# Four graph layers on one core: a bias, a norm and a mask of the last stage in other places

## The chip, the cores and the metric

The kernel runs on one core of a Trainium2 chip. The metric is the device time of one execution in microseconds; the runs shown are the median of three. The engines are called as in the profile: PE (TensorE matmuls, with PEld for its weight loads), DVE (VectorE), ACT (ScalarE), POOL (GpSimd) and SP (SyncE, which issues the transfers).

## What is computed

The input is 128 small graphs of 128 nodes with 128 features, and a 0/1 adjacency matrix for each. Four layers follow each other, every one on a normed and rectified copy of its input, and every one added back to it. The last two are attention layers:

```python
def _L2_gnn_ref(x, adj, W, b, a):          # 4 heads of 32
    h = (x @ W + b).reshape(Bb, Nn, H, D)
    e = e_i[:, :, None, :] + e_j[:, None, :, :]      # h times the halves of a
    e = jnp.where(e > 0, e, 0.2 * e)
    e = jnp.where(adj[..., None] > 0, e, NEG)
    attn = jax.nn.softmax(e, axis=2)
    out = jnp.einsum('bijh,bjhd->bihd', attn, h)
...
def _L3_gnn_ref(h, adj, W, a):             # one head of 128
    ...                                    # the same without b
    return jax.nn.elu(h_prime)

# layers 2 and 3
h = jnp.maximum(_layernorm(x, axis=-1), 0.0)
x = x + _L2_gnn_ref(h, adj, ...)
h = jnp.maximum(_layernorm(x, axis=-1), 0.0)
x = x + _L3_gnn_ref(h, adj, ...)
```

Layer 0 sums over neighbours, and layer 1 is an attention whose scores come from the pairwise differences of all nodes; it takes most of the time. Two batch norms over all graphs stand in layer 1, so the work falls into three stages.

## The kernel before, in words

The 128 graphs are worked in 32 groups of G = 4; a tile of a group is 128 partitions by 4 x 128. The first stage does layer 0 and the pairwise products of layer 1, up to the first batch norm. The second stage reads these products back, forms the scores and attention of layer 1, and gathers the second batch norm. It also prepares, in `brief`, the small constants of the last stage. The last stage does the rest of layer 1 and layers 2 and 3. It comes in two forms: `attention` for the inputs at hand, and `last_stage`, a fallback that a branch takes for others and that does not run here.

`attention(n_th, g, fourth)` breaks one group into some 60 named steps, each with an engine, a planning cost and the names of the steps that it follows. `_ranked` then lists the steps of all groups in one order for each engine: a step is chosen when its predecessors, its buffers (`BUFS`, and the PSUM banks `ONE` and `TWO`) and its engine are free in the plan, ties and near choices being settled by a rank. The rank of a step is `EVERY * n_th + RANK3[name]`, and `JOIN3[n_th]` is the planned time from which a group may start. The engines then run their lists in that order, each instruction waiting for its own inputs.

The steps that matter here, in the order of one group:

- `off` (POOL, L1474): the mask of missing edges from the byte matrix `M8[g]`, 1 where there is no edge. PE multiplies it by `no_edge` and adds the product to the scores (L1619, L1659).
- `y`, `yl`, `po`, `x1`: the end of layer 1; ACT scales, DVE rectifies, PE multiplies, DVE adds (L1477 to L1488).
- `layer(2, ...)` and later `layer(3, ...)`: `mv` takes the moments on DVE (L1501, L1503); `rs` forms the inverse deviation and the negated, scaled mean `nb` on POOL in four small instructions (L231, L232, L1507, L1508); `h` scales and rectifies on ACT in four instructions of 128x128 (L1513); `pt` transposes on PE (L1519), `hT` copies back on ACT (L1588); `pr` multiplies by the weights (L1528), with the two score columns of each head beside the features; `v` copies the score columns out (DVE, L1536) and `wr` the values (ACT, L1551, L1554).
- In layer 2, `pr` starts with two more products for each group, `ones3` by `b_parts` (L1525): the bias, split into three bf16 parts, with its share in the score columns.
- `sp` (POOL, L1567, L1569) splits the scores into three bf16 pieces, `pe` transposes them (L1574), `left` and `right` spread them, and `ps` forms all pair scores (L1616, L1619; L1656, L1659).
- `e` and `em`: two exps on ACT (L1602, L1603) and the larger of them on DVE (L1606); `w` or `pv` multiplies by the values (L1629, L1665); `o` divides by the sums (L1644, L1670). `x2` adds layer 2's result to x, with -1 for the later ELU (L1649); `ex`, `x3`, `x4` and `out` finish layer 3.

`brief` makes `b_parts` in the second stage with its inner functions `joined` and `piece`, twelve small DVE instructions. In the second stage `normed` of `chain` also adds a constant row `bt` to x on POOL (L997) and makes a cap out of the byte matrix by product and sum (L995).

Of the kernel before, what the change touches and what calls it, by code (L numbers as in the profile page):

```python
# [9 lines left out]
F32 = mybir.dt.float32  # L10
I32 = mybir.dt.int32
BF16 = mybir.dt.bfloat16
U8 = mybir.dt.uint8
AF = mybir.ActivationFunctionType
# [50 lines left out]
         ("right3", "right3", "ps"), ("e", "e", "pv"), ("o3", "o", "ex x3"), ("ex", "ex", "x4"))  # L65
EVERY = 16.7
RANK3 = {"off": 260, "y": 228, "yl": 425, "po": 78, "x1": -85, "mv2": 311, "rs2": 127, "h2": 106, "pt2": -67,
         "hT2": -32, "pr2": 29, "v2": -191, "w12": 226, "wr2": -506, "sp2": 154, "pe2": -472, "left2": -44,
         "right2": -400, "ps0": -41, "e0": -28, "e0m": -161, "w0": 61, "e1": 118, "e1m": -270, "w1": 25,
         "o1": -270, "ps2": -33, "e2": 78, "e2m": 74, "w2": 73, "e3": -271, "e3m": -457, "w3": -134, "o3": 98,  # L70
         "x2": -10, "mv3": -52, "rs3": -133, "h3": 71, "pt3": -106, "hT3": 27, "pr3": 92, "v3": -161, "w13": -36,
         "wr3": 125, "sp3": -261, "pe3": -83, "left3": 4, "right3": -32, "ps": -287, "e": 21, "em": -17,
         "pv": -160, "o": -8, "ex": 360, "x3": 119, "x4": 187, "out": 299, "lz": 146, "lx": -73}
JOIN3 = (20, 2, 0, 0, 1, 2, 28, 29, 0, 13, 49, 23, 67, 94, 51, 151,
         131, 78, 137, 199, 221, 127, 166, 143, 241, 183, 223, 276, 237, 165, 178, 294)

# [93 lines left out]
def tile_gnn_stack(ctx: ExitStack, tc: tile.TileContext, a: dict, out: bass.AP):  # L170
# [10 lines left out]
    def fixed(shape, dtype=F32, name=None):  # L181

        if name not in K:
            K[name] = const.tile(shape, dtype, name=name)
        return K[name]
# [78 lines left out]
    def over_group(t):  # L264
        return t[:, None, :].to_broadcast([P, G, P])

    def two_stages(general):
# [535 lines left out]
        with tc.tile_pool(name="c1", bufs=1, reuse_waits="tile") as c1, \  # L803
                tc.tile_pool(name="p1", bufs=2, reuse_waits="tile") as p1:
            prepared, scored = {}, {}
            room["turns"] = p1
            small_ones, pair = [], []
# [74 lines left out]
            def at(slot, place, work):  # L882
                jobs.setdefault((slot, place), []).append(work)
# [206 lines left out]
            no_edge = fixed([P, P], BF16, name="no_edge")  # L1090
            b_parts = fixed([3, P + 8], BF16, name="b_parts")
            ones3 = fixed([3, P], BF16, name="ones3")
            own_h = fixed([P, 4], F32, name="own_h")
            own_k = fixed([P, 4], F32, name="own_k")

            def brief():
# [3 lines left out]
                def scratch():  # L1100
                    for left, names in ((selfb.rearrange("p g t -> p (g t)"),
                                         (("wt0", P), ("wt1", P), ("left", P + 8), ("add_b", 8), ("bounds", 24),
                                          ("square", 16), ("bound", 1), ("by_batch", 16), ("tops", NG + 3))),
                                        (c1.tile([P, P + 8 + 3 * (P // 2 + 4)], F32, name="brief"),
                                         (("part", P + 8), ("one0", P // 2 + 4), ("one1", P // 2 + 4), ("one2", P // 2 + 4)))):
                        for name, n in names:
                            t[name], left = left[:, 0:n], left[:, n:]
                    nc.gpsimd.memset(t["bounds"], 0.0)
                    nc.gpsimd.memset(t["part"], 0.0)
                    nc.gpsimd.memset(ones3, 1.0)  # L1110
                    nc.vector.tensor_copy(ident_b, ident)
                    nc.vector.tensor_scalar(no_edge, ident, NEG_EDGE, None, op0=OP.mult)

# [7 lines left out]
                def copied():  # L1121
                    for i in range(2):
                        nc.scalar.copy(t[f"wt{i}"], t["pt"][:, i, :])
                    nc.scalar.copy(t["add_b"], t["pt"][:, 2, 0:8])

# [16 lines left out]
                def compared():  # L1142
                    nc.vector.tensor_copy(t["bounds"][:, 0:10], t["pn"][:, 0, 0:10])
                    nc.vector.tensor_tensor(t["bounds"][:, 16:24], t["add_b"], t["add_b"], OP.mult)
                    nc.vector.tensor_reduce(t["bound"], t["bounds"], AX.X, OP.max)
# [21 lines left out]

                def joined():
                    nc.vector.tensor_copy(t["left"][0:3, 0:P], b_2[0:3, :])
                    nc.vector.tensor_copy(t["left"][0:3, P:], t["add_b"][0:3, :])  # L1170


                def piece(n):
                    left, part, one = t["left"][0:3, :], t["part"][0:3, :], t[f"one{n}"].bitcast(BF16)[0:3, 0:P + 8]
                    nc.vector.tensor_copy(one, left)
                    nc.vector.tensor_tensor(left, left, one, OP.subtract)
                    nc.vector.scalar_tensor_tensor(part, one, ident[0:3, n:n + 1], part, op0=OP.mult, op1=OP.add)
                    if n == 2:
                        nc.vector.tensor_copy(b_parts, part)

                def owners():
# [12 lines left out]
                at(end + 4, "l", compared)  # L1198
                at(end + 1, "l", joined)
                for n in range(3):  # L1200
                    at(end + 5 + n, "l", lambda n=n: piece(n))
                at(end + 8, "l", owners)
# [30 lines left out]
    w2x, w3x, wtyT, b_2, b_2c, a2, a3, ident_b, no_edge, \  # L1233
        ones3, b_parts, own_h, own_k, scale2, bias2, bounded, flag = (
        K[n] for n in ("w2x", "w3x", "wtyT", "b_2", "b_2c", "a2", "a3", "ident_b", "no_edge", "ones3", "b_parts", "own_h", "own_k", "scale2", "bias2", "bounded", "flag"))

    def last_stage():
        nonlocal psum, banks
        with tc.tile_pool(name="c2", bufs=1) as c2, tc.tile_pool(name="p2", bufs=5) as p2, \
# [84 lines left out]
            def group(g):  # L1324
# [7 lines left out]
                off = p2.tile([P, G, P], BF16, name="off")  # L1332
                nc.gpsimd.tensor_scalar(off, M8[g], 0.0, None, op0=OP.is_equal)
                yield
# [47 lines left out]

                nc.vector.scalar_tensor_tensor(x, o, -1.0, x, op0=OP.add, op1=OP.add)
                yield
# [38 lines left out]
    with tc.If(nc.values_load(bounded, min_val=0, max_val=1) > 0) as cmp, \  # L1423
# [10 lines left out]
        def attention(n_th, g, fourth):  # L1434
# [38 lines left out]
            def masked():  # L1473
                nc.gpsimd.tensor_scalar(sb("off", [P, G, P], BF16), M8[g], 0.0, None, op0=OP.is_equal)  # L1474

            step("off", "Pool", 1.54, lx, masked)
            step("y", "ACT", 0.81, () if on_chip else ("lz",), lambda: nc.scalar.activation(  # L1477
# [13 lines left out]
            def layer(n, heads, wx, first):  # L1491
# [18 lines left out]
                def normed():  # L1510
                    h = sb("h", [P, G, P])
                    for k in range(G):
                        nc.scalar.activation(h[:, k, :], t["x"][:, k, :], AF.Relu, bias=t[nb][:, k:k + 1],  # L1513
                                             scale=t[rs][:, k:k + 1])
# [6 lines left out]
                def projected():  # L1521
                    pr = two(q("pr"), N)
                    if first:
                        for a in range(2):
                            nc.tensor.matmul(pr[:, a, :, :], ones3, b_parts[:, None, :].to_broadcast([3, 2, N]),  # L1525
                                             start=True, stop=False, skip_group_check=True)
                    for k in range(G):
                        nc.tensor.matmul(pr[:, k // 2, k % 2, :], t[q("hT")][:, k, :], wx, start=not first,  # L1528
                                         stop=True, skip_group_check=True)

                def scores():
                    v = sb(q("v"), [P, 2, G, heads])
                    for a in range(2):
                        v_a = v[:, :, 2 * a:2 * a + 2, :].rearrange("p s b h -> p b s h")
                        pr_a = t[q("pr")][:, a, :, P:].rearrange("p b (s h) -> p b s h", s=2)
                        nc.vector.tensor_copy(v_a, pr_a)  # L1536

# [41 lines left out]
                def right():  # L1579
# [5 lines left out]
                step(rs, "Pool", 1.85, (mv,), root)  # L1585
                step(q("h"), "ACT", 1.65, (rs,), normed)
                step(q("pt"), "PE", 0.65, (q("h"),), turned, takes=(q("pt"),))
                step(q("hT"), "ACT", 0.59, (q("pt"),), lambda: nc.scalar.copy(sb(q("hT"), [P, G, P]), t[q("pt")]),  # L1588
                     last=(q("pt"),))
                step(q("pr"), "PE", 1.50 if first else 1.15, (q("hT"),), projected, takes=("2" + q("pr"),))  # L1590
                step(q("v"), "DVE", 0.32, (q("pr"),), scores)
# [17 lines left out]
            for k in range(G):  # L1609
# [38 lines left out]

            step("x2", "DVE", 0.69, ("o3",), lambda: nc.vector.scalar_tensor_tensor(  # L1649
                t["x"], t["o2"], -1.0, t["x"], op0=OP.add, op1=OP.add))  # L1650

# [86 lines left out]
```

## Time and profile before

| | before |
|---|---|
| median of 3 runs | 2656.92 us (2652.68 to 2657.95) |
| the profiled execution | 2653.83 us |
| its span | 2652.0 us |
| last stage, from the first `y` to the last result on DVE | 2225.5 to about 2647 us |

The span is what the profiler sees between the first and the last instruction; the execution's own time is 1.8 us longer. A group row of the profile gives the line, the engine, the operation, output and input names with their sizes and the count; behind the first bar the busy time and the mean of one in ns, behind the second the idle time of the engine just before, and whose work ended it. A window row gives each engine's busy time and instructions in a stretch, the granted PE clock, the DMA share and the GB/s moved. A wait row says which engine waited at which line for which other, with total, count and longest. A row with three figures in ns gives the shortest, median and longest instruction.

### The profile page before, as it was taken

Reading aid. Unit: us, or ns where it says so; the run is one execution under the profiler, and the core shown is the slowest. Engines: PE = TensorE matmul, PEld = TensorE weight load, DVE = VectorE, ACT = ScalarE, POOL = GpSimd, SP = SyncE. Lnnn points to the kernel's source line nnn. Section 1 sums busy time; section 2 is a strip of 40 time slices with the busy share of each in tenths; the row PEclk is TensorE's granted clock in tenths of the full one; section 3 lists DMA queues with packets and bytes.
Section 4 is the critical chain, followed back from the end, with each engine's and each line's share of the span. In section 5 each row is a group of like instructions: output and inputs, shape, how many; then the busy total and the mean of one; then the engine's idle time right before and its main releaser. Section 6 shows DMA issues by size and latency. Waiting matters only on the chain. (4 is left out here: it accounts for less than half of the span.)

```text
span 2652.0 us, 41948 instructions
## 1 busy us (share of the span) xinstructions
PE 2425.3 (91%) x14521; PEld 1155.4 (44%) x14521; DVE 2468.8 (93%) x4740; ACT 2376.6 (90%) x2821; POOL 1693.7 (64%) x1628
## 2 busy tenths in 40 slices
PE   6999999999999999999998988888888887999997
PEld 3333333333333333333332444444444445777776
DVE  5999999999999999999998898888888897899997
ACT  5999999999999999999998978887777774999997
POOL 6999999999999999999996110101110014666663
PEclk8999999999999999999999999999999997999999
DMA  3555555555555555555556899999999982021211
GB/s 102 199 207 210 209 212 207 214 208 211 207 210 207 210 207 210 207 210 210 207 210 227 339 408 410 409 410 409 410 409 410 398 345 81 21 69 57 66 36 34
DMA packets 185426, 611.43 MB, mean 231 GB/s; under 512 B 31987, under 2 KB 99702, under 8 KB 121718
## 3 DMA queue, kind: packets, MB, share of 16 engines
q1 hardware_dynamic: 184768, 608.50, 59.8%
q8 instruction: 118, 1.93, 0.3%
q14 instruction: 102, 0.84, 0.1%
q10 hardware_dynamic: 438, 0.17, 0.0%
HBM read 312.58 MB, written 296.03 MB: 229 GB/s over the span
## 5 line engine op out<-in xcount | busy, mean ns | idle before, releaser
L328 POOL TENSOR_TENSOR d<-xe 128x2048 f32<-128x2048 f32 x256 | 1073.5, 4203 | 36.5 <-PE hp L338 34.5
L338 PE MATMUL hp<-d,w1T 128*64 128x512 f32 x4096 | 994.2, 601 | 57.0 <-ACT z L352 54.0
L376 ACT ACTIVATE d<-d 128x2048 f32<-128x2048 f32 x384 | 733.5, 1922 | 20.2 <-POOL d L328 19.8
L328 DVE TENSOR_TENSOR d<-xe,xp 128x2048 f32<-128x2048 f32 x256 | 580.1, 2266 | 6.9 <-POOL xe L423 4.0
L352 ACT COPY z<-hp 128x1024 f32<-128x1024 f32 x512 | 519.0, 1015 | 9.7 <-PE hp L338 4.6
L338 PEld LDWEIGHTS hp<-d,w1T 128*64 128x64 f32 x4096 | 277.2, 136 | 558.7 <-issue 454.7
L997 POOL TENSOR_TENSOR x<-x,bt 128x512 f32<-128x512 f32 x27 | 39.1, 1449 | 555.6 <-DMA x<-x 447.7
L366 DVE BATCH_NORM_STATS2 st<-z 128x6 f32<-128x512 f32 x512 | 347.6, 679 | 6.1 <-ACT z L352 6.0
L367 DVE BATCH_NORM_STATS2 st<-z 128x6 f32<-128x512 f32 (+1 forms) x512 | 329.2, 643 | 0.0
L945 DVE SCALAR_TENSOR_TENSOR z<-z 128x2048 f32<-128x2048 f32 x128 | 297.8, 2327 | 6.3 <-ACT z L915 6.3
L926 ACT ACTIVATE zr<-z,bias,scale 128x2048 f32<-128x2048 f32 x128 | 267.3, 2089 | 7.8 <-DVE bias L797 7.8
L915 ACT ACTIVATE z<-z,bias,scale 128x2048 f32<-128x2048 f32 x128 | 267.0, 2087 | 0.0
L341 PE MATMUL hp<-both_t,xw 128*64 128x512 f32 x1024 | 265.2, 592 | 0.0
L892 PE MATMUL ps<-z,w2z 128*32 128x512 f32 x1024 | 139.5, 616 | 65.1 <-DVE z L945 64.8
L899 PEld LDWEIGHTS pk<-pick,su 128*128 128x128 f32 x1024 | 124.0, 191 | 138.1 <-DVE su L913 105.9
L899 PE MATMUL pk<-pick,su 128*128 128x16 f32 x1024 | 136.4, 265 | 25.5 <-DVE su L913 24.9
L892 PE MATMUL ps<-z,w2l 128*32 128x512 f32 x1024 | 139.7, 607 | 2.1 <-DVE w2l L853 2.1
L341 PEld LDWEIGHTS hp<-both_t,xw 128*64 128x64 f32 x1024 | 77.6, 137 | 142.1 <-issue 142.1
L892 PE MATMUL ps<-zr,w2r 128*32 128x512 f32 x1024 | 139.0, 608 | 0.0
L1629 PE MATMUL pv<-wr,e 128*128 128x128 f32 x1024 | 134.0, 278 | 2.0 <-ACT wr L1554 1.1
L1629 PEld LDWEIGHTS pv<-wr,e 128*128 128x128 f32 x1024 | 124.1, 192 | 8.3 <-ACT wr L1554 1.7
L1606 DVE SCALAR_TENSOR_TENSOR e<-e,ps 128x512 f32<-128x512 f32 x160 | 106.7, 674 | 10.7 <-ACT ps L1603 10.3
(257 smaller groups left out, 3788.7 us busy)
## 6 DMA issues: line engine op xcount, KB each, us to landing
hp<-z SPq DMA_DIRECT2D x248, 1024.0 KB, 4.0
z<-hp SPq DMA_DIRECT2D x248, 1024.0 KB, 13.0
x<-x SPq DMA_DIRECT2D x118, 256.0 KB, 5.4
u<-rows SPq DMA_DIRECT2D x32, 384.0 KB, 11.5
x<-in_x_dram SPq DMA_DIRECT2D x32, 256.0 KB, 5.6
adj<-in_adj_dram SPq DMA_DIRECT2D x32, 256.0 KB, 5.9
z<-y SPq DMA_DIRECT2D x27, 256.0 KB, 11.8
y<-z SPq DMA_DIRECT2D x27, 256.0 KB, 2.8
```

Of the source, the lines that this page charges most:

```text
L328: eng.tensor_tensor(d, ahead, x[:, None, None, :].to_broadcast([P, 2, KC, P]), OP.max if t == BY_MAX else OP.subtract)
L338: nc.tensor.matmul(hp[64 * hh:64 * hh + 64, c:c + 512], w1T2 if by_max else w1T, d[:, hh, c:c + 512], start=True, stop=not by_max, skip_gr ...
L341: nc.tensor.matmul(hp[64 * hh:64 * hh + 64, c:c + 512], XW[i // NT // 2][:, i // NT % 2, :], both_t.rearrange("p h k i -> p h (k i)")[:, h ...
L352: nc.scalar.copy(half_of(b, t), linear.pop(i))
L366: nc.vector.bn_stats(st[:, 2 * t, :], hs[:, 0:512])
L367: nc.vector.bn_stats(st[:, 2 * t + 1, :], hs[:, 512:1024 - P * last])
L376: nc.scalar.activation(diffs[i], diffs[i], AF.Abs)
L892: nc.tensor.matmul(ps[32 * c:32 * c + 32, :], w[:, w0:w0 + 32], v[:, 512 * c:512 * c + 512], start=start, stop=stop, skip_group_check=True)
L899: nc.tensor.matmul(pk[:, kk, 0:16], su[:, kk, :], pick.rearrange("p h j -> p (h j)"), start=True, stop=True)
L915: linear = lambda z: nc.scalar.activation(z, z, AF.Identity, bias=bias1, scale=scale1[:, 0:1])
L926: nc.scalar.activation(zr, z1, AF.Relu, bias=bias1, scale=scale1[:, 0:1])
L945: nc.vector.scalar_tensor_tensor(z0, z0, 0.01, z0, op0=OP.mult, op1=OP.max)
```

## The change

Four things change in the last stage, and its constants with them.

- The bias of layer 2 is no longer added by products in `pr`. Its share in the scores is added by DVE in `v` (`add_b`); its share in the values, which the softmax passes on unchanged because its weights sum to one, is added to x itself by a new step `xb` on POOL after `h2`. `x2` becomes a plain addition; the -1 goes into `bt` once, at the start of the second stage.
- `h3` moves from ACT to POOL, as x times `rs` plus `nb`; the rectifying goes into `hT3`.
- `off` is made as byte times 1 plus -1, so that a missing edge is -1, and `no_edge` changes its sign.
- `EVERY`, `RANK3` and `JOIN3` have new values, and so each engine's order of steps is another one throughout the stage.

`joined` and `piece` of `brief` go. The fallback is changed in the same sense; it does not run.

```diff
-EVERY = 16.7
-RANK3 = {"off": 260, "y": 228, "yl": 425, "po": 78, "x1": -85, ...
+EVERY = 18.0
+RANK3 = {"off": 165, "y": 582, "yl": 244, "po": 343, "x1": 51, ...
 ...
+            if not general:
+                nc.gpsimd.tensor_scalar(bt, bt, -1.0, None, op0=OP.add)
 ...
-                    nc.vector.tensor_scalar(no_edge, ident, NEG_EDGE, None, op0=OP.mult)
+                    nc.vector.tensor_scalar(no_edge, ident, -NEG_EDGE, None, op0=OP.mult)
 ...
-                nc.gpsimd.tensor_scalar(sb("off", [P, G, P], BF16), M8[g], 0.0, None, op0=OP.is_equal)
-
-            step("off", "Pool", 1.54, lx, masked)
+                nc.gpsimd.tensor_scalar(sb("off", [P, G, P], BF16), M8[g], 1.0, -1.0, op0=OP.mult, op1=OP.add)
+
+            step("off", "Pool", 0.8, lx, masked)
 ...
-                    for k in range(G):
+                    for k in range(G * (not first)):
+                        nc.gpsimd.tensor_scalar(h[:, k, :], t["x"][:, k, :], t[rs][:, k:k + 1], t[nb][:, k:k + 1],
+                                                op0=OP.mult, op1=OP.add)
+                    for k in range(G * first):
                         nc.scalar.activation(h[:, k, :], t["x"][:, k, :], AF.Relu, bias=t[nb][:, k:k + 1],
                                              scale=t[rs][:, k:k + 1])
 ...
-                    if first:
-                        for a in range(2):
-                            nc.tensor.matmul(pr[:, a, :, :], ones3, b_parts[:, None, :].to_broadcast([3, 2, N]),
-                                             start=True, stop=False, skip_group_check=True)
                     for k in range(G):
-                        nc.tensor.matmul(pr[:, k // 2, k % 2, :], t[q("hT")][:, k, :], wx, start=not first,
-                                         stop=True, skip_group_check=True)
+                        nc.tensor.matmul(pr[:, k // 2, k % 2, :], t[q("hT")][:, k, :], wx, start=True, stop=True)
 ...
-                        nc.vector.tensor_copy(v_a, pr_a)
+                        if first:
+                            add = add_b.rearrange("p (s h) -> p s h", s=2)[:, None, :, :]
+                            nc.vector.tensor_tensor(v_a, pr_a, add.to_broadcast([P, 2, 2, heads]), OP.add)
+                        else:
+                            nc.vector.tensor_copy(v_a, pr_a)
 ...
-                step(q("h"), "ACT", 1.65, (rs,), normed)
+                step(q("h"), *(("ACT", 1.65) if first else ("Pool", 2.1)), (rs,), normed)
 ...
-                step(q("hT"), "ACT", 0.59, (q("pt"),), lambda: nc.scalar.copy(sb(q("hT"), [P, G, P]), t[q("pt")]),
+                step(q("hT"), "ACT", 0.59, (q("pt"),), lambda: nc.scalar.activation(
+                    sb(q("hT"), [P, G, P]), t[q("pt")], AF.Copy if first else AF.Relu),
                      last=(q("pt"),))
-                step(q("pr"), "PE", 1.50 if first else 1.15, (q("hT"),), projected, takes=("2" + q("pr"),))
+                step(q("pr"), "PE", 1.15, (q("hT"),), projected, takes=("2" + q("pr"),))
 ...
-            step("x2", "DVE", 0.69, ("o3",), lambda: nc.vector.scalar_tensor_tensor(
-                t["x"], t["o2"], -1.0, t["x"], op0=OP.add, op1=OP.add))
+            step("xb", "Pool", 1.28, ("h2",), lambda: nc.gpsimd.tensor_tensor(t["x"], t["x"], over_group(b_2), OP.add))
+            step("x2", "DVE", 0.69, ("o3", "xb"), lambda: nc.vector.tensor_tensor(t["x"], t["o2"], t["x"], OP.add))
```

## Prediction

> **What bounds the kernel now.** I read the page's busy line first, then the windows of the last stage, then its groups, then its waits. The edits that move work lie in the last stage, so the whole-span shares only say that three engines are near full everywhere:
>
> ```profile
> PE 2425.3 (91%) x14521; PEld 1155.4 (44%) x14521; DVE 2468.8 (93%) x4740; ACT 2376.6 (90%) x2821; POOL 1693.7 (64%) x1628
> ```
>
> The stage runs from the first `y` on ACT at 2225.5 us to about 2649, 423.5 us for 32 groups. Cut in head, middle and tail (windows; busy us and instructions of each engine):
>
> ```profile
> core 0: us, PE busy (x) PEld busy (x) DVE busy (x) ACT busy (x) POOL busy (x), PEclk, DMA share, GB/s
> 2225.50:2250.00 24.50, 17.63 (x96) 15.46 (x96) 16.23 (x66) 15.88 (x37) 19.89 (x47) 0.70 0.22 73
> 2250.00:2600.00 350.00, 333.19 (x2542) 264.69 (x2542) 322.29 (x1043) 329.97 (x781) 222.20 (x609) 1.00 0.16 48
> 2600.00:2649.00 49.00, 37.99 (x277) 29.94 (x276) 38.41 (x109) 33.50 (x81) 14.90 (x56) 0.91 0.14 40
> ```
>
> In the middle PE is busy 95%, ACT 94%, DVE 92%, POOL 63%: no single bound, three engines in step. The stage's sums over 32 groups give each engine's work per group: PE 388.8/32 = 12.15 us, ACT 379.4/32 = 11.85, DVE 376.9/32 = 11.78, POOL 257.0/32 = 8.03. At PE's 12.15 the middle's 333.2 us hold 27.4 groups, a pace of 12.8 us, so the fullest engine is 95% full. The groups that the change touches, in the window from 2220 us on (busy, mean ns, idle before and who ended it):
>
> ```profile
> L1513 ACT ACTIVATE h<-x,nb,rs 128x128 f32<-128x128 f32 x216 | 89.0, 489 | 13.3 <-POOL nb L1508 11.7 <-POOL wr L1545 1.3
> L1513 ACT ACTIVATE h<-z,nb,rs 128x128 f32<-128x128 f32 x40 | 16.5, 490 | 7.3 <-POOL nb L1508 7.2
> L1474 POOL TENSOR_SCALAR off<-m 128x512 bf16<-128x512 uint8 x32 | 50.5, 1584 | 16.0 <-PE ps L1659 11.7 <-DVE mv L1503 4.3
> L1525 PE MATMUL pr<-b_parts,ones 3*128 3x272 bf16 x64 | 12.8, 279 | 0.5 <-ACT wr L1551 0.3 <-DVE o L1670 0.2
> L1536 DVE COPY v<-pr 128x16 f32<-128x16 f32 x64 | 7.8, 162 | 6.1 <-PE pr L1528 4.7 <-POOL pieces L1567 0.9 <-PE pt L1519 0.5
> ```
>
> How much of POOL's idle time is real? Its waits between 2250 and 2600 us, the four longest (total, times, longest):
>
> ```profile
> POOL rs L231 <- DVE mv L1503: 38.7, 15, 7.6
> POOL pieces L1567 <- DVE v L1536: 21.1, 13, 4.4
> POOL off L1474 <- PE ps L1659: 11.7, 5, 3.9
> POOL rs L231 <- DVE v L1536: 9.3, 5, 5.2
> ```
>
> All the listed waits sum to 95.5 us, so POOL is held 350 - 95.5 = 254.5 us, not 222: the gaps between its small instructions count. Per group that is 254.5/27.4 = **9.3 us held**, and this is the number to carry forward.
>
> **What the Trainium skill says.** *GPSIMD Engine Reference*, section 3.1, prices a two-input elementwise operation on GpSimd at nearly twice VectorE's time. The trace agrees: 4203 against 2266 ns for 2048 elements (L328), and 1272 ns (median of L997) against 675 for 512. *Perfetto Trace Analysis*, section "GPSIMD Engine Instruction", says to time GpSimd by start-to-start spacing, not by reported duration; that is why I use 9.3. *SBUF - State Buffer*, section "Who interferes with whom", says that a VectorE instruction with two SBUF inputs and a GpSimd instruction that reads SBUF shut each other out. The rows agree on one side (min/median/max of one instruction):
>
> ```profile
> L1508 POOL TENSOR_SCALAR nb<-nb x64: 237/238/1217, 2235.5 to 2630.4; 128x4 f32<-128x4 f32 x64
> L1649 DVE SCALAR_TENSOR_TENSOR x<-o,x x27: 678/683/741, 2294.7 to 2626.4; 128x512 f32<-128x512 f32 x27
> L995 POOL TENSOR_SCALAR cap<-m x32: 617/942/2546, 1481.4 to 2195.0; 128x512 f32<-128x512 uint8 x32
> L997 POOL TENSOR_TENSOR x<-x,bt x27: 1263/1272/3345, 1490.9 to 2105.4; 128x512 f32<-128x512 f32 x27
> ```
>
> GpSimd stretches up to five times; the VectorE row hardly moves.
>
> **Part by part, per group.**
>
> *Third norm from ACT to POOL.* L1513 has 256 instructions and 105.5 us; half leave ACT: 52.7/32 = -1.65 us. POOL gains four 128x128 product-and-sum instructions with two pointer operands, not in the trace. Lower bound: the same kind with constants costs 238 ns at 4 elements and 617 at 512 (L1508, L995), so about 0.33 us at 128; a copy of that size takes 289 ns (L423). Upper: with GpSimd's two-input slope, (1272 - 199)/508 = 2.1 ns an element, 0.47; the diff's planner prices the four at 2.1, 0.53 each. With the 0.08 us gap seen between small instructions: 1.6 to 2.5; I take **+2.3**. Behind it on POOL wait the next group's `rs`, split (`sp`) and mask; PE's transposes wait for it as they did for ACT. The Relu moves into `hT3`: 585 ns now, at most 632 (the exp of L1679); hidden by the freed ACT.
>
> *Bias out of the product.* PE loses two 3x272 products: 12.80/32 = **-0.40** (their loads overlap). `xb` on POOL is L997's operation and shape: 1272 median, 1449 mean, with a gap **+1.4** (1.3 to 1.9). It waits for `h2`, and `x2` waits for it, but four exps, the products and `o3` lie between; it is off the chain unless POOL falls that far behind. `v2` on DVE becomes an addition: 2 x 162 ns, to at most 2 x 200, **+0.05**. `x2` as a plain addition: L1488 is one, 675 against 687: nothing.
>
> *Mask by product and sum.* 1584 ns becomes L995's kind of operation: 617 undisturbed, 942 median beside the 2.3 us VectorE instructions of the stage before; here such instructions last 0.68, so 0.75: **-0.8** (-0.6 to -1.0).
>
> *Set-up.* The split of the bias (12 small DVE instructions in the second stage) goes, one small POOL instruction on `bt` comes. At the end of that stage the DMA share is 1.02 (2100 to 2150 us), so DVE's 2 us are hidden by the transfers; without that cover up to -2. SP's transfers stay.
>
> *Sums.* PE 12.15 - 0.40 = 11.75; DVE 11.78 + 0.05 = 11.83; ACT 11.85 - 1.65 = 10.2; POOL held 9.3 + 2.3 + 1.4 - 0.8 = **12.2** (11.2 to 13.3). ACT's relief is paid by POOL nearly one for one. The fullest engine was PE at 12.15 of 12.8; now POOL, DVE and PE are at 11.75 to 12.2. I let POOL be held 98% (part of its 9.3 is blocking, which is not fixed) and the other two 95%: 12.4 to 12.45 us a group. The middle gives 0.35 to 0.4 x 27.4, some -10; because no queue has slack I keep **-6**.
>
> *Order, head and tail.* Read from the instruction lists: before, POOL has five masks ahead of its first `rs2`, and the first mask-free `rs` starts at 2233.7 us; ACT has 20 steps ahead of its first exps. After, two masks stand ahead, group 0 runs ahead of the others, and the first exps have 12 steps ahead: worth about **-3** of the 24.5 us head (0 to -5). In the tail the last six groups each need rs3, h3 and the split on POOL, 1.9 + 2.3 + 1.4 = 5.6 us, where DVE needs 5.2 (1.26 + 0.3 + 0.7 + 0.7 + 0.9 + 0.7 + 0.7): **0** (-3 to +6).
>
> Together -9 us. The profiled execution took 2653.83 us (span 2652.0 and 1.8 around it): 2645. The median of the runs shown is 3.1 higher, so 2648.
>
> **Rivals.** (1) *POOL becomes the pacing queue, slower.* Place: h3 and xb ahead of `sp` and `rs` in POOL's list. From 12.5 us held per group on (0.98 of the old pace) it decides. With h3 at 0.6, xb at 1.9 through blocking by yl, x2, x3, x4 (four two-input VectorE instructions, 2.7 us a group), POOL is at 9.3 + 2.7 + 1.9 - 0.7 = 13.2, pace 13.4, +0.6 x 27.4 = +17: 2674. For it: L997's 3345 and L1508's 1217; against: L1508's mean, 313, is still near its median. (2) *Nothing gained.* DVE is the same 11.8 as before, and `rs` and `sp` already wait on DVE for most of POOL's idle time; what ACT gives is waited for elsewhere: 2655. (3) *All of it.* If h3 costs 0.33, POOL is at 11.5 and the pace follows DVE at 96%: 12.3, -14 and -3 and -3 in the tail: 2637. (4) Should the mask keep its 1.58 us in the new form, POOL gets 0.8 more and ends in (1).
>
> **Numbers.** About 0.2% (5.3 us) is what a measurement of this kernel tells from no change. Forecast 0.44, its own range 2640 to 2651; all of it 0.12; nothing gained 0.17; POOL paces 0.27. So faster 0.44 + 0.12 = 0.56. The range from 2632 to 2674 leaves out the far end of (1) and a gain beyond (3).
>
> **What would show it.** Right: L1525's rows gone; ACT near 80% in the middle with new waits on POOL or PE; POOL busy 80 to 90%; h 0.45 to 0.6 us each; off about 0.75; DVE and PE 95%; stage about 414 us. Wrong: POOL above 92% busy with PE waiting for `pieces` or h (rival 1); a stage over 425; or DVE's x rows above 0.75 us, contention on the side where before shows none.

## The result, and the profile after

The changed kernel takes 2669.75 us (median of 6 runs, 2664.48 to 2675.17) against 2652.43 us for the kernel before in the same rounds: a ratio of 1.0062, interval 1.0042 to 1.0083. It is slower by some 17 us, where -9 was forecast. The profiled execution took 2671.18 us with a span of 2669.4, 17.4 more than the span before.

The busy line of the page, to be held against the one before:

```profile
PE 2429.4 (91%) x14457; PEld 1162.0 (44%) x14457; DVE 2479.4 (93%) x4728; ACT 2332.2 (87%) x2693; POOL 1771.7 (66%) x1787
```

ACT lost 44 us and 128 instructions, POOL gained 78 and 159. PE lost its 64 products and is not less busy. The last stage in three windows, now 2225.0 to about 2664 us (busy us and instructions of each engine, granted clock, DMA share, GB/s):

```profile
core 0: us, PE busy (x) PEld busy (x) DVE busy (x) ACT busy (x) POOL busy (x), PEclk, DMA share, GB/s
2225.00:2250.00 25.00, 18.66 (x104) 16.28 (x105) 17.83 (x69) 15.58 (x34) 19.20 (x45) 0.68 0.07 22
2250.00:2600.00 350.00, 319.18 (x2393) 257.88 (x2392) 314.43 (x1010) 284.57 (x657) 280.99 (x738) 0.98 0.17 49
2600.00:2665.00 65.00, 52.75 (x356) 40.71 (x354) 51.70 (x139) 36.37 (x80) 32.14 (x89) 0.86 0.11 30
```

In the middle PE fell from 95 to 91%, DVE from 92 to 90, ACT from 94 to 81, and POOL rose from 63 to 80. No engine is full, and PE, DVE and ACT do less in the same time. The waits of the middle say what they wait for (waiting engine and line, who ended it, total, times, longest), first before the change:

```profile
PEld L1574 <- POOL pieces L1567: 9.4, 13, 1.4
...
PE pe L1574 <- POOL pieces L1567: 5.0, 6, 1.2
...
ACT left L1596 <- PE pe L1574: 2.8, 5, 0.8
```

Then after it:

```profile
PEld L1554 <- POOL pieces L1547: 17.8, 18, 2.0
ACT left L1577 <- PE pe L1554: 15.6, 21, 1.5
...
POOL rs L232 <- DVE mv L1481: 13.4, 8, 3.4
...
PE pe L1554 <- POOL pieces L1547: 10.6, 12, 1.7
```

Before, POOL waited for `mv` 38.7 us in that window; now 13.4. PE's waits for POOL's split (`pieces`) have doubled, and ACT's `left` waits for the transpose behind it. All of POOL's listed waits sum to 34.7 us, so its queue is held 315.3 of 350 us, **90%**; before it was 73%. The profile also gives the chain of work that ended last, followed back from the last instruction, at each step to what released it. In the middle 34% of this chain now lies on POOL and 6% on ACT; before it was 18% and 16%.

The groups that changed (busy, mean ns, idle before):

```profile
L1491 POOL TENSOR_SCALAR h<-x,rs,nb 128x128 f32<-128x128 f32 x108 | 54.0, 512 | 0.6
L1630 POOL TENSOR_TENSOR x<-x,b 128x512 f32<-128x512 f32 x27 | 35.8, 1327 | 1.2 <-ACT h L1494 1.2
L1452 POOL TENSOR_SCALAR off<-m 128x512 bf16<-128x512 uint8 x32 | 21.0, 661 | 3.0 <-PE ps L1640 2.9
L1457 DVE SCALAR_TENSOR_TENSOR y<-y 128x512 f32<-128x512 f32 x27 | 20.4, 764 | 0.2 <-ACT y L1455 0.2
L1631 DVE TENSOR_TENSOR x<-o,x 128x512 f32<-128x512 f32 x27 | 20.1, 743 | 0.1
L1466 DVE TENSOR_TENSOR x<-x,po 128x512 f32<-128x512 f32 x27 | 18.2, 675 | 0.9 <-PE po L1463 0.7
```

Every POOL price lies near its forecast. The DVE instructions with two inputs in SBUF, 682 and 687 ns before, now take 764 and 743; the one that reads one input from PSUM (L1466) is still at 675.

Four landmarks in the trace cut the stage better than round windows: its first `y` on ACT, the first and the last product of layer 2 with the values (`w`, 32 to a group), and the end of the last `x4` on DVE. Head, middle and tail between them, in us, from one profiled execution of each kernel:

| kernel | head | middle | tail | sum |
|---|---|---|---|---|
| before | 29.0 | 370.8 | 21.5 | 421.3 |
| after | 22.0 | 384.8 | 32.3 | 439.2 |
| difference | -7.0 | +14.0 | +10.8 | +17.8 |

In the tail the chain that ended last runs through POOL for nine microseconds (start us, us, what):

```profile
2636.51 0.21 POOL pieces L1547
...
2638.41 0.25 POOL rs L232
2638.73 1.05 POOL rs L233
...
2641.16 0.69 POOL v L1549
2641.90 0.73 POOL pieces L1547
2642.63 1.72 POOL h L1491 x4
...
2645.40 0.20 POOL pieces L1547
2645.65 0.39 PE pe L1554 x2
```

Split, `rs`, another split, `h3`, another split: the last group's norm stands among the splits of the groups before it. When the last layer-2 product is issued, six groups still have their layer-3 products with the values ahead of them; in the kernel before it was four.

### The profile page after: what moved, and what is told of

It reads as the page before. It is cut to its first block, busy times and chain, and to the rows that moved or that the text cites. A ratio compares the mean times of both kernels' runs of the same rounds, so it can differ in the third digit from the quotient of the medians.

```text
span 2669.4 us, 41840 instructions
## 1 busy us (share of the span) xinstructions
PE 2429.4 (91%) x14457; PEld 1162.0 (44%) x14457; DVE 2479.4 (93%) x4728; ACT 2332.2 (87%) x2693; POOL 1771.7 (66%) x1787
## 5 line engine op out<-in xcount | busy, mean ns | idle before, releaser
L902 PE MATMUL pk<-pick,su 128*128 128x16 f32 x1024 | 137.4, 266 | 20.6 <-DVE su L916 20.4
L1610 PE MATMUL pv<-wr,e 128*128 128x128 f32 x1024 | 141.4, 283 | 2.8 <-ACT wr L1531 1.0
L1610 PEld LDWEIGHTS pv<-wr,e 128*128 128x128 f32 x1024 | 128.8, 196 | 12.1 <-ACT wr L1534 2.0
L1587 DVE SCALAR_TENSOR_TENSOR e<-e,ps 128x512 f32<-128x512 f32 x160 | 107.2, 676 | 13.3 <-ACT ps L1584 12.8
```

What stands on the lines that cost most here:

```text
L902: nc.tensor.matmul(pk[:, kk, 0:16], su[:, kk, :], pick.rearrange("p h j -> p (h j)"), start=True, stop=True)
L1610: nc.tensor.matmul(t[pv][:, k % 2, hd, :], t[e][:, hd, :], flat[:, at:at + P], start=True, stop=True)
```

## The experiments

In what follows "order held" means that the planner's engines, costs and ranks are those of the kernel named, so that the list of steps is the same, and only what a step issues is changed. Kernels whose names begin with b have the old order, those with a or i the new one. Ratios are to the kernel before, on the same chip.

**b_all.** All three edits of work in the old order.

```diff
 # kernel before: EVERY, RANK3, JOIN3 and the costs unchanged
+ off by product and sum; h3 on POOL, Relu in hT3; bias out of pr, add_b in v
+ w12: memsets of wr2, then gpsimd.tensor_tensor(x, x, over_group(b_2), OP.add)
```

> All three edits of work (bias out of the product, third norm on POOL, mask by product and sum) in the order of the kernel before, step for step; the bias addition on POOL is issued with the step w12. Theory 'load' (POOL's added work and its blocking with DVE cost the time, whatever the order): about as slow as the changed kernel or slower, ratio to before 1.004 to 1.012, POOL held over 90% in the middle. Theory 'order' (the edits are worth a few us, the newly searched order loses more): ratio 0.994 to 1.001.

2698.09 us, ratio 1.0175 (1.0161 to 1.0189). The edits lose 46 us where the order was made for other work, more than 'load' had asked for. POOL is held 85% there, and 41% of the middle's chain lies on it. With these edits the new order is the better one: it takes 28 of the 46 us away.

**a_none.** The new order with the old work.

```diff
-            step("xb", ..., lambda: nc.gpsimd.tensor_tensor(t["x"], t["x"], over_group(b_2), OP.add))
+            step("xb", ..., lambda: None)      # and off, h3, pr, v, x2 as before
```

> The new order with the work of before: mask by comparison, third norm on ACT and bias in the product, each issued at its place in the new order, the bias addition left empty. Theory 'order': slower than before by 15 us or more, ratio over 1.005. Theory 'load': ratio 0.998 to 1.003, since POOL is as free as before.

2674.29 us, 1.0075 (1.0061 to 1.0089). An order fits its own work: the old work in the new order loses 22 us too, here with POOL held 71% and ACT busy 316 of 350 us; 45% of the middle's chain lies on ACT and 10% on POOL. So neither theory holds alone; order and work go together.

**a_h3act.** The changed kernel with h3 issued on ACT (and `hT3` a plain copy again).

```diff
-                        nc.gpsimd.tensor_scalar(h[:, k, :], t["x"][:, k, :], t[rs]..., t[nb]..., op0=OP.mult, op1=OP.add)
+                        nc.scalar.activation(h[:, k, :], t["x"][:, k, :], AF.Relu, bias=t[nb]..., scale=t[rs]...)
```

> The changed kernel with only the third norm's scaling issued on ACT again, at the same place of the order. Theory 'load': POOL is held 9.8 us a group, and the 17 us come back, ratio to before 0.995 to 1.001. Theory 'order': ratio 1.004 to 1.010, as ACT is filled again and the order stays.

2673.43 us, 1.0079 (1.0065 to 1.0092). POOL is freed to 76% and nothing is won: 1.65 us a group went to ACT's list, and 37% of the middle's chain now lies on ACT, where the changed kernel has 6. It takes a kernel that frees POOL and fills nobody to tell.

**b_h3.** The kernel before with h3 on POOL alone: the same lines as in the diff of the change, without `xb`, mask and bias.

> The kernel before with only the third norm's scaling issued on POOL, at its place in the old order. Theory 'load': POOL held 9.3 + 2.3 = 11.6 us a group; slower by 5 to 15 us, ratio 1.002 to 1.006. Theory 'order': ACT is freed by 1.65 us a group and nothing else moves; ratio 0.996 to 1.001.

2686.19 us, 1.0132 (1.0117 to 1.0148). 34 us where 5 to 15 were expected, with POOL held only 82%. The chain tells more than the held share: 35% of the middle's chain lies on POOL, as in the changed kernel. In an order not made for it, a step on POOL can be late even with a fifth of the queue empty.

**a_h3q.** A quarter of h3, order held.

```diff
-                    for k in range(G * (not first)):
+                    for k in range(1 * (not first)):
...
-                        nc.tensor.transpose(pt[:, k, :], t["h"][:, k, :], ident)
+                        nc.tensor.transpose(pt[:, k, :], t["h"][:, k * first, :], ident)
```

> The changed kernel with three of the four instructions of the third norm's scaling left out (the transposes read the first one's result four times): POOL loses 1.65 us a group, nothing comes to another engine, the order is held. If POOL's load or its place in the chain sets the pace in the new order: 12 to 20 us faster than the changed kernel, ratio to before 0.997 to 1.002. If the order itself is the loss: ratio 1.004 to 1.008.

2654.27 us, 1.0005 (0.9995 to 1.0014). Nearly the whole loss is gone: the middle is 370.5 us, and the tail's longer time is made up by the shorter head.

**a_xb8.** The bias addition on 8 of 128 columns, order held.

```diff
-nc.gpsimd.tensor_tensor(t["x"], t["x"], over_group(b_2), OP.add)
+nc.gpsimd.tensor_tensor(t["x"][:, :, 0:8], t["x"][:, :, 0:8], over_group(b_2)[:, :, 0:8], OP.add)
```

> The changed kernel with the bias addition on POOL over 8 of the 128 columns: POOL loses about 1.0 us a group, and its longest blocking instruction; order held. If load: 6 to 12 us faster than the changed kernel, ratio to before 1.001 to 1.004. If the order: ratio 1.005 to 1.008.

2652.79 us, 0.9998 (0.9988 to 1.0009). More than expected: one microsecond of work a group on POOL (1276 ns to 250, medians) is worth 17. The middle is 367.3 us, 17.5 shorter than in the changed kernel; the tail stays at 32.3.

**a_tail6.** h3 of the last six groups on ACT, order held.

```diff
-                    for k in range(G * (not first)):
+                    for k in range(G * (not first and n_th >= 26)):
+                        nc.scalar.activation(h[:, k, :], t["x"][:, k, :], AF.Identity, bias=t[nb]..., scale=t[rs]...)
+                    for k in range(G * (not first and n_th < 26)):
```

> The changed kernel with the third norm's scaling of the last six groups alone issued on ACT, at the same places of the order. After the last layer-2 product the changed kernel needs 32 us to its end and the kernel before 21.5; in the chain of waits POOL holds 9 of them (rs, split, h, split). If POOL in the tail is that loss: 6 to 11 us faster than the changed kernel, ratio to before 1.002 to 1.004. If not: ratio 1.005 to 1.008.

2667.17 us, 1.0050 (1.0031 to 1.0069). This lies between the two expectations, and its interval overlaps that of the changed kernel. In the trace the tail shrinks from 32.3 to 27.8 us, still 6 above before, so h3 on POOL is less than half of the tail's loss. With the old work in the new order (a_none) the tail is 30.2, with a quarter of h3 on POOL (a_h3q) 30.3; in every kernel with the old order it is 21.5 to 27.3. The rest goes with the new order, which leaves layer 3 of six groups behind the last layer-2 products where the old one leaves four.

**b_off.** The mask alone in the old order.

```diff
-nc.gpsimd.tensor_scalar(sb("off", ...), M8[g], 0.0, None, op0=OP.is_equal)
+nc.gpsimd.tensor_scalar(sb("off", ...), M8[g], 1.0, -1.0, op0=OP.mult, op1=OP.add)    # and the sign of no_edge
```

> The kernel before with the mask by product and sum alone, in the old order. POOL loses 0.9 us a group and nothing is added. If POOL's position is part of what limits the old order too: 3 to 8 us faster, ratio 0.997 to 0.999. If POOL has slack there: ratio 0.999 to 1.001.

2650.45 us, 0.9990 (0.9979 to 1.0000). On the border between the two expectations, with an interval that reaches 1. POOL goes from 73 to 67% and little follows.

**a_memset.** a_xb8 with two memsets behind the small addition.

```diff
+                nc.gpsimd.memset(unread, 0.0)      # unread: 128 x 450, never read
+                nc.gpsimd.memset(unread, 0.0)
```

> The kernel a_xb8 (bias addition on 8 of 128 columns, which took the 17 us away) with two memsets of 450 elements behind it on POOL, about 1.0 us together, that only write: POOL is held as long as in the changed kernel, but reads nothing in that time. If held time of POOL's queue is what counts: back to ratio 1.005 to 1.008. If the shutting out between POOL's reads and DVE's two-input instructions counts: ratio 0.999 to 1.002.

2670.55 us, 1.0061 (1.0047 to 1.0074). The loss is back though POOL reads nothing in that time. The profiled execution was the fastest of the five, 2657.75 us; even so its middle is 379.7 against 367.3. The row of `x2` in it:

```profile
L1638 DVE TENSOR_TENSOR x<-o,x 128x512 f32<-128x512 f32 x27 | 18.6, 688 | 0.1
```

688 ns, not the 743 of the changed kernel (695 in a_xb8): the shutting out on DVE is gone and the time is not. In this order what counts is how long POOL's queue is held, not what POOL reads meanwhile.

**a_biasin.** The new order with the bias in the product and `xb` empty, h3 on POOL, mask by product and sum.

> The changed kernel with the bias back in the product and no addition on POOL, order held: third norm on POOL, mask by product and sum. POOL loses 1.35 us a group, PE gets 0.33 back. If POOL's load is the loss: ratio 0.999 to 1.003, near a_xb8. If PE is as tight as POOL: ratio 1.003 to 1.006.

2652.97 us, 1.0004 (0.9994 to 1.0013). PE takes the bias products back (12.9 us over the stage, 0.40 a group) without harm, 96% busy in the middle; POOL is held 81%.

**a_both.** The cuts of a_h3q and a_xb8 together.

> The changed kernel with three quarters of the third norm's scaling and 120 of 128 columns of the bias addition left out, order held; POOL held about 9.5 us a group as before the change. If POOL still paces in a_xb8 and a_h3q: another 8 to 15 us, ratio 0.994 to 0.997. If another engine or the tail paces by then: ratio 0.998 to 1.001.

2639.61 us, 0.9945 (0.9932 to 0.9958). With POOL loaded about as before the change, ACT and PE relieved and the new order kept, the kernel is 13 us faster than before: the middle is 356.2 us, the tail still 30.2. This leaves work out, so it is what the relief would be worth if nobody had to pay for it. Only 13% of the middle's chain lies on POOL, and 53% on DVE.

**b_bias.** The bias out of the product alone, in the old order: the same lines as in b_all for the bias.

> The kernel before with the bias out of the product alone, in the old order; the addition on POOL is issued with step w12, ahead of the split. If POOL's held time and blocking count in any order: slower by 8 to 20 us, ratio 1.003 to 1.008. If PE's 0.33 us a group outweighs it: ratio 0.996 to 1.000.

2676.71 us, 1.0094 (1.0079 to 1.0108). More than expected. In the old order the addition stands behind `h2`, ahead of the split, and there its time counts; 36% of the middle's chain lies on POOL. Another place in that order was not tried.

**a_nb.** h3 from the moments themselves, `nb` not formed in layer 3; `mv3` gets five buffers instead of two, the plan stays.

```diff
-                        nc.gpsimd.tensor_scalar(h[:, k, :], t["x"][:, k, :], t[rs]..., t[nb]..., op0=OP.mult, op1=OP.add)
+                        nc.gpsimd.tensor_scalar(h[:, k, :], t["x"][:, k, :], t[mv][:, k, 0:1], t[rs]..., op0=OP.subtract, op1=OP.mult)
```

> The changed kernel with the third norm on POOL as x minus mean, times rs, from the moments themselves, so that the two small instructions that form nb (0.29 + 0.27 us from start to start) go in layer 3; order and everything else held, the whole computation done. If POOL's held time paces (17 us for 1.35 us a group so far, 12 us per us): 5 to 9 us faster than the changed kernel, ratio to before 1.003 to 1.005. If it was the place of the bias addition alone: ratio 1.005 to 1.008.

2690.25 us, 1.0147 (1.0133 to 1.0161): 20 us above the changed kernel, where 5 to 9 below it were expected. One instruction of h3, shortest, median and longest, in the changed kernel and then in a_nb:

```profile
L1491 POOL TENSOR_SCALAR h<-x,rs,nb x108: 440/448/1485, 2333.4 to 2643.9; 128x128 f32<-128x128 f32 x108
```
```profile
L1492 POOL TENSOR_SCALAR h<-x,mv,rs x108: 787/794/2298, 2332.3 to 2657.9; 128x128 f32<-128x128 f32 x108
```

Product and sum takes 448 ns, difference and product 794. By these medians four of them are 1.4 us more, and the two small instructions saved are 0.56, so POOL got some 0.8 us a group more, not less (1.2 by its held time), and the time followed.

**a_lean, i_lean.** a_nb, and a_biasin with the same h3, each with the constant columns of `wr2` and `wr3` set once in fixed buffers. The buffers are taken in a fixed turn, which is not that of the plan and changes part of the values.

```diff
-                        wr = sb(q("wr"), [P, G + 1, 4, 33])
-                        nc.gpsimd.memset(...)      # three in a group
+                    t[q("wr")] = ring[taken_by[heads] % len(ring)]
```

> As a_nb, and the constant columns of wr2 and wr3 are set once in fixed buffers instead of in each group (three memsets a group less, some 0.4 us from start to start). If POOL's held time paces: 9 to 15 us faster than the changed kernel, ratio 1.001 to 1.003. Otherwise 1.005 to 1.008.

> As a_lean, with the bias back in the product (a_biasin was level with before): POOL loses another 1.0 us a group against a_biasin. If POOL still paces there, as a_both says: 8 to 13 us faster than before, ratio 0.995 to 0.997. If PE or DVE has taken over: ratio 0.998 to 1.001.

a_lean 2688.79 us, 1.0131 (1.0115 to 1.0148); i_lean 2666.19 us, 1.0045 (1.0029 to 1.0061). Both miss what was expected, since both carry the slow h3; i_lean is 13 us above a_biasin. Among the others they lie where POOL's held time puts them (table below).

**b_lean.** b_off with the constant columns set once, in the old order.

> The kernel before, in its order, with the mask by product and sum and the constant columns set once; POOL loses 1.3 us a group of its 9.3, nothing is added. If POOL's held time counts in any order: 8 to 15 us faster, ratio 0.995 to 0.997. If it counts only where POOL is full: ratio 0.998 to 1.000, like the mask alone (0.999).

2649.76 us, 0.9988 (0.9981 to 0.9995). POOL is held 65% and the gain is 3 us. In the old order, where 18% of the middle's chain lay on POOL, more slack is worth next to nothing. Of the versions that leave no work out, this is the one that beats both kernels beyond its interval, by a tenth of a per cent.

**i_ring, i_half.** a_biasin with the constant columns set once, a buffer being taken again when its last product is issued; and with two of the four instructions of h3 on ACT besides.

```diff
+                    for k in range(2 * (not first)):
+                        nc.scalar.activation(h[:, k, :], t["x"][:, k, :], AF.Identity, bias=t[nb]..., scale=t[rs]...)
+                    for k in range(2 * (not first), G * (not first)):
```

> The new order with the third norm on POOL (product and sum), the mask by product and sum and the bias in the product (a_biasin, level with before), and the constant columns of wr2 and wr3 set once in fixed buffers: three memsets a group less, some 0.4 us of POOL. If POOL's held time paces: 4 to 7 us faster than a_biasin, ratio to before 0.997 to 0.999. If not: 0.999 to 1.002.

> As i_ring, with two of the four instructions of the third norm issued on ACT and two on POOL, order held: POOL loses another 1.05 us a group, ACT gets 0.8 of the 1.65 back. If POOL's held time paces and ACT has slack at 11 us a group: 8 to 14 us faster than before, ratio 0.994 to 0.997. If ACT is as tight as POOL in this order: ratio 0.998 to 1.003.

i_ring 2653.39 us, 0.9999 (0.9991 to 1.0007); i_half 2656.31 us, 1.0005 (0.9994 to 1.0017). Neither gains. i_ring's POOL is held 9.87 us a group against a_biasin's 9.75, although three memsets of 0.41 us together are gone; the runs do not show why, so i_ring does not test a shorter queue. i_half's POOL is down to 73% and ACT up to 90% busy; 8% of the middle's chain lies on POOL and 32% on ACT, where a_biasin has 13 and 13. The 0.8 us given to ACT eat what POOL wins.

Over the kernels in the new order that keep ACT relieved, the middle follows the held time of POOL per group. Held is 350 us less POOL's waits between 2250 and 2600, divided by the groups in that window, counted by layer-2 products (28.8 before, 27.1 after). The last column is POOL's part of the chain in that window:

| kernel | POOL held per group, us | share of the window | middle, us | part of the chain |
|---|---|---|---|---|
| a_both | 8.45 | 75% | 356.2 | 13% |
| a_biasin | 9.75 | 81% | 368.0 | 13% |
| i_ring | 9.87 | 82% | 367.3 | 17% |
| a_h3q | 10.04 | 82% | 370.5 | 20% |
| a_xb8 | 10.16 | 85% | 367.3 | 22% |
| i_lean | 10.92 | 86% | 380.0 | 32% |
| a_memset | 11.39 | 90% | 379.7 | 38% |
| after | 11.62 | 90% | 384.8 | 34% |
| a_tail6 | 11.64 | 90% | 386.5 | 37% |
| a_lean | 12.53 | 93% | 399.2 | 51% |
| a_nb | 12.84 | 93% | 401.5 | 51% |

From a_xb8 to a_nb it is 34 us for 2.7 us of POOL, 12.8 us for each. If POOL alone set the pace, one microsecond a group would cost 32 us over 32 groups. The part of the chain fits with its being less: from a_xb8 to a_nb the chain lies on POOL for a fifth to a half of the middle, and on the other engines for the rest. The table shows no mark below which POOL costs nothing: between a_both and a_biasin, at 75 and 81%, there are already 12 us.

## Why the prediction was wrong

- **The middle: the step that failed is "I let POOL be held 98% and the other two 95%".** The sum took the fullest engine, let it run nearly without a wait, and so charged POOL's added work only as far as it made POOL the fullest. In the trace POOL is held 90%, PE is busy 91% and DVE 90%, and none of them reaches what it was allowed. Counted as the forecast counted, by PE's busy time over its work per group, the changed kernel does 319.2/12.2 = 26.2 groups in the window: POOL is held 12.1 us a group, forecast 12.2, but the pace is 13.4, forecast 12.4. So the load was right and the share was not. POOL still waits 34.7 us there, above all for DVE, while PE waits 10.6 us and its weight loads 17.8 us for POOL's split: a queue can be late for others and still have waits of its own. The prices were right: h3 4 x 0.51 forecast 0.45 to 0.6, `xb` 1.33 forecast 1.3 to 1.9, mask 0.66 forecast 0.75. (The upper end of POOL's sum should read 13.1, not 13.3.) a_memset, which holds POOL without reading anything, shows that in this order it is the held time that counts.
- **The unit of the pace.** I divided PE's work over the whole stage into the middle and got 27.4 groups and 12.8 us. Counted by layer-2 products it is 28.8 and 12.15. This did not turn the sign: in that count POOL is held 8.8 us before, 11.7 with what was forecast to come, and at 98% the pace would be 12.0, still a gain of some 5 us. It halves the gain that the sum gave, and it moves the point from which the first rival had POOL decide from 12.5 to 11.9. The runs show no such point.
- **Rival 1 is the case that came**, in place and sign: PE waiting for `pieces`, the split behind h3 and `xb`. Its time, 2674, is near the 2669.75 by luck: it put 17 us into the middle and took h3 at 0.6 and `xb` at 1.9, while the measured prices are 0.51 and 1.33 and the loss is 14 us in the middle and 11 in the tail, less 7 in the head. Its sign, POOL above 92% busy, did not come either: POOL is 80% busy and 90% held. Its mechanism has one part too many: the blocking between POOL and DVE does happen, and on DVE's side as well, where I had said that the row hardly moves. 50 to 80 ns on four instructions a group are some 7 us of DVE busy time over the stage, but a_memset takes it away and leaves the loss. One of the four is `x2`: I priced it at 675 ns from L1488, which has an input in PSUM; with both in SBUF it takes 743.
- **ACT and PE.** ACT is at 81% as forecast. PE's 0.40 us a group did not come out of its busy time: 390.6 us over the stage against 388.8, since other products took longer (those of `w` 141.4 us against 134.0). In a_both, where PE's clock stays at 1.00 through the middle, the sum is 377.2, and there the gain is real (13 us).
- **Head:** forecast -3 from the shorter list ahead of the first exps, measured -7.0. It comes with the new order: 20.6 to 22.6 us in every kernel that has it, 28.0 to 31.5 in those with the old one. Right in sign, and beyond the range of 0 to -5.
- **Tail:** forecast 0, at most +6; measured +10.8. I compared POOL's 5.6 us a group with DVE's 5.2 for six groups in both orders, and did not see that the new order leaves layer 3 of six groups to the end where the old one leaves four. a_tail6 puts 4.5 us of it on h3; with h3 back on ACT (a_tail6, a_none, a_h3act) 6 to 9 us remain, and they go with the order.
- **Set-up:** hidden, as forecast: the stage starts at 2225.0 against 2225.5.

Left open: whether another order of the changed work would be faster than before; none was tried.

## What to carry to other kernels

An engine can set the time well before its busy time says so: POOL was 80% busy, the least of the four, when one microsecond less on it was worth 17. Count the time between its waits, and see how much of the chain lies on it; in these kernels the chain named the engine that mattered also where the held share did not (POOL in b_h3, ACT in a_none). Do not price an engine in such a sum as if it could run nearly without waits. Work moved from an engine that is one of three full ones to the fourth is not free while the fourth has slack, and the receiving list needs a place for it: the same edits lost 46 us in the old order and 17 in one made for them. When a unit of pace is taken from a trace, use the same count on both sides of the comparison.

## What the runs showed of the hardware that was not expected

- On POOL operations of one shape differ in price. For 128x128 in f32 with two pointer operands, product and sum takes 448 ns, difference and product 794 (a_nb; its operands differ too, so the operation alone was not separated). For the mask, 512 bytes a partition, a comparison takes 1505 ns (median) and product and sum 617, before and after:

```profile
L1474 POOL TENSOR_SCALAR off<-m x32: 1479/1505/1982, 2226.3 to 2550.1; 128x512 bf16<-128x512 uint8 x32
```
```profile
L1452 POOL TENSOR_SCALAR off<-m x32: 612/617/1142, 2225.9 to 2572.9; 128x512 bf16<-128x512 uint8 x32
```

- The Trainium skill's *SBUF — State Buffer*, section "Who interferes with whom", says that a GpSimd instruction that only writes does not contend with a two-input VectorE instruction. a_memset agrees: `x2` takes 688 ns there, 695 without the memsets (a_xb8), and 743 in the changed kernel, where POOL reads in that time. The row with an input in PSUM stays at 675 and 674.
- PE's granted clock was 1.00 through the whole middle before. After the change it has four stretches of 3.4 us at half clock there. The Trainium skill's *TensorE: Matmul & The Clock Gate*, Part 1, describes a clock that halves after an idle window of about 3.4 us. This trace agrees in part: PE was not idle in the 3.4 us ahead of these stretches but busy 39 to 56%, and in three of the four it waited there 1.5 to 2.1 us for POOL. Cut into such stretches of 3.4 us, the middle of the kernel before never falls below 64%. As an estimate from the trace, 13.7 us at half clock cost PE at most 6.8 us of work; and since a_xb8, with a middle 17.5 us shorter, still has 10.2 us at half clock, the clock is not what separates the two.
